# The lower block of a symmetric pair as the transposed image of the upper one, in a graph-convolution kernel

## The chip, the cores and the metric

The kernel runs on one core of one Trainium2 chip. The metric is the device time of one execution in microseconds (us), lower is better. A core has five engines that run side by side, each with its own queue in order: TensorE (PE, with its weight loads as PEld), VectorE (DVE), ScalarE (ACT), GpSimd (POOL) and SyncE (SP, which here only starts DMAs). ACT and POOL start DMAs as well. Matrix products and transposes end in PSUM, and DVE or ACT copies them out to SBUF. The core's DMAs share 16 DMA engines.

## The reference

```python
HW = jnp.einsum('bnf,fo->bno', H, W)            # H = x: (8, 4096, 256), W: (256, 256)
A_norm = jax.nn.relu((A + A.T) * 0.5)           # A = adj: (4096, 4096)
D = jnp.sum(A_norm, axis=1)
d_inv_sqrt = jnp.where(D > 0, D_safe ** (-0.5), 0.0)
DAD = d_inv_sqrt[:, None] * A_norm * d_inv_sqrt[None, :]
L_norm = jnp.eye(N, dtype=H.dtype) - DAD
out = jax.nn.relu(jnp.einsum('nm,bmo->bno', L_norm, HW))
x = layernorm(x + out, axis=-1)
```

All of it is float32. `A_norm` is symmetric: its block (j, i) is the transpose of its block (i, j).

## The kernel before

The work has two stages. The first makes `A_norm`, writes it to DRAM (`a_dram`), makes the rows of HW scaled by their degree (`g`), writes them too (`g_dram`), and forms the first 128 rows of the product on the way (`lead`). The second gathers rows of `g_dram` and pieces of `a_dram` by lists of indices, multiplies them, adds x, normalises and stores the output. The change touches the first stage alone.

**The pair loop (L718 to L768).** A is cut in 8 by 8 blocks of 512x512. A row i of blocks runs j from i to 7; a pair i < j needs two loads of 1 MB on SP, `adj[i,j]` and `adj[j,i]` (L505, four buffers). There are 8 diagonal blocks and 28 pairs: row i has 7 - i pairs. `symmetrise` (L511) makes one block of the sum: for each of its four groups of 128 rows, four 128x128 transposes on PE (L515) fill one PSUM bank (`tr`, of the tag `b0`, four banks), and one addition on DVE (L519) adds the other block out of SBUF and writes 512 columns of `sym`. For a pair it runs twice, once for (i, j) and once for (j, i): 32 transposes and 8 additions. `sym` has three buffers of 1 MB.

**Beside it** run two more things, traced after the two `symmetrise` (L742). `multiply` (L582) is four products of 512 columns for each strip that is ready; they go to four banks of their own. `form` (L595) makes 128 rows of `g`: it loads two pieces of x (L608, or L574 on POOL), transposes them on PE (L615, 16 transposes in four banks of `b0`), copies each bank out on ACT (L616), multiplies by W (L626, 32 products in four banks of `b0`), and copies each bank out on ACT (L636 or L638).

**`keep` (L522)** then runs for each of the two blocks: ACT applies `relu(0.5 * sym)` in place over 2048 columns (L523), DVE sums groups of 32 columns (L526) and those sums again (L531), POOL notes which groups are not empty (L527), ACT starts the store of 1 MB to `a_dram` (L532). `run_due` (L675) after each `keep` does a due piece of work on the index lists, nearly all of it many short DVE instructions with a few products (L241 to L419). It is thickest in rows 2 to 4. During rows 3 and 5 one `sym` buffer is lent to a list (`hot`, L705).

**The order.** A framework puts the traced instructions in each engine's queue ahead of the run, the earlier traced first among those that its own estimate holds ready; the queue itself then runs strictly in order and waits on semaphores. So the queues aren't in the order of the code: additions of the next pair can stand ahead of sums of this one. `tc.issue_after` pins one instruction behind another on its engine (L743, in the last row).

Of the kernel before, what the change touches and what calls it, by code (L numbers as in the profile page):

```python
# [9 lines left out]
F32 = mybir.dt.float32  # L10
AF = mybir.ActivationFunctionType
# [56 lines left out]
def kernel(  # L68
# [25 lines left out]
    nc = tc.nc  # L94
    B, N, F = x.shape
    FO = w.shape[1]
    P = 128
    S = 512
    A = S // P
# [20 lines left out]
    def blocks(u):  # L120

        return min(2, NB - 1 - 2 * u)
# [23 lines left out]
    ident = const.tile([P, P], F32, name="ident")  # L146
# [20 lines left out]
    psum = ctx.enter_context(tc.tile_pool(name="psum", bufs=4, space=bass.MemoryType.PSUM))  # L167
# [322 lines left out]
    with (  # L490
# [12 lines left out]
        def load_adj(i, j):  # L503
            t = blocks_pool.tile([P, A, S], F32, tag="adj", name=f"adj_{i}_{j}")
            nc.sync.dma_start(  # L505
                t,
                adj[i * S : (i + 1) * S, j * S : (j + 1) * S].rearrange("(a p) s -> p a s", p=P),
            )
            return t

        def symmetrise(i, j, tij, tji, sym):  # L511
            for a in range(A):
                pt = psum.tile([P, S], F32, tag="b0", name=f"tr_{i}_{j}_{a}")
                for c in range(A):
                    ins = nc.tensor.transpose(  # L515
                        pt[:, c * P : (c + 1) * P], tji[:, c, a * P : (a + 1) * P], ident
                    )
                done_pe.append(ins.ins)
                nc.vector.tensor_add(sym[:, a, :], pt, tij[:, a, :])  # L519
                yield  # L520

        def keep(i, j, sym, diag):  # L522
            nc.scalar.activation(sym, sym, AF.Relu, scale=0.5)  # L523
            rows = slice(i * A, (i + 1) * A)
            sums = stat1.tile([P, A, S // E], F32, tag="sums", name=f"sums_{i}_{j}", bufs=3)
            nc.vector.tensor_reduce(sums, sym.rearrange("p a (c q) -> p a c q", q=E), AX.X, ALU.add)  # L526
            ins = nc.gpsimd.tensor_scalar(  # L527
                uses[:, rows, j * S // E : (j + 1) * S // E], sums, 0.0, None, ALU.is_gt
            )
            flags.append(ins.ins)  # L530
            nc.vector.tensor_reduce(part[:, rows, j], sums, AX.X, ALU.add)  # L531
            nc.scalar.dma_start(  # L532
                a_dram[i * S : (i + 1) * S, j * S : (j + 1) * S].rearrange("(a p) s -> p a s", p=P), sym
            )
            if i == j:
                for a in range(A):
                    nc.gpsimd.tensor_copy(diag[:, a, :], sym[:, a, a * P : (a + 1) * P])
# [44 lines left out]
        def multiply(m, g, strip):  # L582
            for c in range(G // S):
                nc.tensor.matmul(  # L584
                    lead[c],
                    lhsT=strip,
                    rhs=g[:, c * S : (c + 1) * S],
                    start=not done,
                    stop=len(done) == NB - 1,
                    skip_group_check=True,  # L590
                )
                yield
            done.append(m)
# [63 lines left out]
        def release_all(i):  # L657
            for m in range(i * A, (i + 1) * A):
                if m in held:
                    release(m)  # L660
            lower_diagonal(i, diags.pop(i))
# [5 lines left out]
        def quota(i, j):  # L667

            if i in (2, 3) and j == i:
                return 0  # L670
            return int(j > i or i > 3)
# [3 lines left out]
        def run_due(flush=False):  # L675
            for d in due:
                d[0] -= 1
            while due and (flush or due[0][0] <= 0):
                _, fn, args = due.pop(0)
                fn(*args)  # L680
# [37 lines left out]
        for i in range(NS):  # L718
            diag = stat1.tile([P, A, P], F32, tag="diag", name=f"diag_{i}")
            for j in range(i, NS):  # L720
                tij = load_adj(i, j)
                tji = load_adj(j, i) if j > i else tij
                parts = [(i, j, tij, tji)] + ([(j, i, tji, tij)] if j > i else [])
                parts = [(p, spool.tile([P, A, S], F32, tag="sym", name=f"sym_{p[0]}_{p[1]}")) for p in parts]
                beside = [multiply(*args) for args in waiting]
                waiting.clear()
                products = len(beside)

                for _ in range(quota(i, j)):
                    if known:  # L730
                        beside.append(form(known.pop(0), True, i >= 4))
                    elif early:
                        beside.append(form(early.pop(0), False))
                for p, sym in parts:
                    for _ in symmetrise(*p, sym):
                        pass
                if i == NS - 1:


                    release_all(i - 1)  # L740
                    beside = beside[products:] + beside[:products]
                for n, b in enumerate(beside):  # L742
                    with tc.issue_after(done_pe[-1]) if i == NS - 1 and n < 2 else nullcontext():  # L743
                        for _ in b:
                            pass
                for (rows, cols, _, _), sym in parts:
                    keep(rows, cols, sym, diag)
                    run_due()
            degrees(i)
            diags[i] = diag  # L750
            if i != NS - 2:
                release_all(i)
            known += range(i * A, min((i + 1) * A, NB - HOLD))
            if i in (1, 2, 3, 4):
                u = SEQ[i - 1]
                at = 4 if i == 4 else 1
                gap = 2 if i == 1 else 1
                due += [[at, patterns, (u,)], [at + 1, count_place, (u,)]]
                due += [[at + 1 + (k + 1) * gap, more, (u,)] for k in range(3)]
                if i < 4:  # L760
                    due.append([at + 2 + 3 * gap, count_place_rest, (u,)])
            if i in (2, 4):
                u = SEQ[i // 2 - 1]
                at = 4 if i == 2 else 0
                pieces = spread_early(u)
                due += [[at + k, next, (pieces, None)] for k in (1, 2, 3, 3, 4)]
                due.append([at + 5, collect_index, (u,)])
            due.sort(key=lambda d: d[0])  # L768
# [204 lines left out]
    with (  # L973
# [292 lines left out]
        for q, (u, step) in enumerate(steps):  # L1266
            new = q == 0 or steps[q - 1][0] != u
            if new:
                prepare(u)
                after(4, classify, u)  # L1270
                rows = [2 * u + 1 + b for b in range(2)] if q > 0 and blocks(u) == 2 else []
# [33 lines left out]
            for c in range(NC):  # L1305
                for op in step:
                    rows = slice(0, P) if op[1] is None else slice(op[1] * L, (op[1] + 1) * L)
                    cols = slice(op[3] * E, (op[3] + op[4]) * E)
# [82 lines left out]
```

## Time and profile before

| | us |
|---|---|
| median of 3 runs | 1469.06 (1465.74 to 1475.9) |
| the profiled execution: its own time | 1471.74 |
| its span, first to last instruction | 1470.0 |
| mean granted TensorE clock | 0.978 of full speed |
| PE busy, share of the span | 1382.5, 94% |
| DVE busy | 1025.7, 70% |
| POOL busy | 735.3, 50% |
| ACT busy | 370.8, 25% |

The first stage ends near 586 us: the last instruction of the pair loop runs near 551 us, and then 80 products of `lead` follow. A busy PE is not PE at its peak, since its products are pipelined and their ends are modelled. A wait is put down to the engine or DMA that came last.

### The profile page before, as it was taken

The page shows a single profiled execution, that of the slowest core. Times are in us where ns is not written, and L with a number is a line of the kernel's source. Part 1 is how long each engine was busy: PE and PEld are TensorE (multiplying, and loading weights), DVE is VectorE, ACT ScalarE, POOL GpSimd, SP SyncE. Part 2 cuts the span into 40 slices and gives each one's busy share as a digit, 9 for nine tenths or more (in the row PEclk, how much of TensorE's full clock was granted, in tenths as well). Part 3 has the DMA queues.
Part 4 walks back from the last instruction along what each step waited for, and adds up shares of the span by engine and source line. Part 5 has one row for each costly group of instructions (what it writes and reads, how often), then busy time and mean ns, then how long its engine had stood idle before and what let it go on. Part 6 is the DMA issues. An engine that isn't in the chain of part 4 may idle for free.

```text
span 1470.0 us, 20174 instructions
## 1 busy us (share of the span) xinstructions
PE 1382.5 (94%) x6584; PEld 744.3 (51%) x6584; DVE 1025.7 (70%) x3020; ACT 370.8 (25%) x462; POOL 735.3 (50%) x1521
## 2 busy tenths in 40 slices
PE   7998998979999999999999999998999999999995
PEld 6777877767777774343334333333333333333432
DVE  4667668879787851538659688788879239999544
ACT  4555455544445451010100101100100010101112
POOL 2335001010214244756767777676667647666663
PEclk9999999989999999999999999999999999999998
DMA  9999999999999999979999999999999979999996
GB/s 351 348 369 371 402 389 333 391 379 341 367 362 359 373 375 391 363 300 378 380 412 356 372 402 408 389 353 389 394 386 361 406 276 398 405 391 408 409 384 233
DMA packets 215008, 545.83 MB, mean 371 GB/s; under 512 B 16983, under 2 KB 106647, under 8 KB 179879
## 3 DMA queue, kind: packets, MB, share of 16 engines
q0 software_dynamic: 53552, 287.25, 49.7%
q1 hardware_dynamic: 93200, 126.62, 24.8%
q10 hardware_dynamic: 68144, 130.58, 23.2%
q8 instruction: 55, 0.90, 0.2%
q14 instruction: 57, 0.47, 0.1%
HBM read 426.33 MB, written 136.34 MB: 383 GB/s over the span
## 4 chain that ended last, share of the span: by engine, by line
PE 49%; DMA 26%; DVE 14%; issue 5%; POOL 3%; ACT 2%; POOLq 0%; ACTq 0%; DVEq 0%; SPq 0%
PE py L1254 28%; DMA g<-g_dram,gi 12%; PE pg L626 9%; DMA a_dram<-sym 6%; PE lead L584 5%; DMA ga<-a_dram,ai 4%; DVE sym L519 4%; PE tr L515 3%; DMA xin<-in_x_dram 3%; PE xtr L615 3%; DVE sums L526 2%; POOL ga L1031 1%; ACT sym L523 1%; POOL g L1039 1%; DVE stats L806 1%
## 5 line engine op out<-in xcount | busy, mean ns | idle before, releaser
L1254 PE MATMUL py<-g,ga 128*128 128x512 f32 (+4 forms) x2808 | 659.7, 603 | 16.9 <-DMA g<-g_dram,gi 16.8
L1254 PEld LDWEIGHTS py<-g,ga 128*128 128x128 f32 (+4 forms) x2808 | 233.5, 140 | 408.6 <-issue 379.0
L1039 POOL DMA_INDIRECT g<-g_dram,gi x257 | 289.8, 1128 | 131.6 <-issue 66.1
L1031 POOL DMA_INDIRECT ga<-a_dram,ai x257 | 271.8, 1058 | 146.3 <-issue 50.6
L787 ACT ACTIVATE y<-py,minus_r 128x512 f32<-128x512 f32 x120 | 82.5, 687 | 764.8 <-PE py L1254 725.3
L626 PE MATMUL pg<-w_sb,xt 128*128 128x256 f32 x1024 | 231.8, 385 | 6.0 <-ACT xt L616 6.0
L626 PEld LDWEIGHTS pg<-w_sb,xt 128*128 128x128 f32 x1024 | 196.0, 194 | 33.4 <-ACT xt L616 6.7
L519 DVE TENSOR_TENSOR sym<-tr,adj 128x512 f32<-128x512 f32 x256 | 162.1, 683 | 58.7 <-PE tr L515 50.4
L526 DVE TENSOR_REDUCE sums<-sym 128x64 f32<-128x2048 f32 x64 | 145.6, 2280 | 67.6 <-ACT sym L523 63.5
L1254 PE MATMUL py<-g_hub,gh 128*128 128x512 f32 x384 | 174.4, 601 | 0.0
L527 POOL TENSOR_SCALAR uses<-sums 128x64 uint8<-128x64 f32 x64 | 26.6, 415 | 272.0 <-DVE sums L526 242.0
L515 PE MATMUL tr<-ident,adj 128*128 128x128 f32 x1024 | 137.4, 281 | 20.1 <-DVE sym L519 19.2
L523 ACT ACTIVATE sym<-sym 128x2048 f32<-128x2048 f32 x64 | 122.7, 1918 | 120.5 <-DVE sym L519 108.0
L515 PEld LDWEIGHTS tr<-ident,adj 128*128 128x128 f32 x1024 | 115.7, 143 | 50.8 <-DVE sym L519 36.6
L241 DVE TENSOR_TENSOR_SCAN incl_r<-carry,lists 128x32 f32<-128x32 bf16 x13 | 2.8, 219 | 171.6 <-PE lists L396 171.6
L1254 PEld LDWEIGHTS py<-g_hub,gh 128*128 128x128 f32 x384 | 70.2, 190 | 97.6 <-issue 82.9
L428 DVE TENSOR_TENSOR hot<-iota_q,at 128x1024 bf16<-128x1024 f32 x64 | 74.5, 1218 | 33.8 <-PE lead L584 31.9
L797 DVE TENSOR_TENSOR xr<-xr,y 128x2048 f32<-128x2048 f32 x31 | 70.9, 2287 | 36.9 <-ACT y L787 36.9
L615 PE MATMUL xtr<-ident,xin 128*128 128x128 f32 x512 | 75.2, 301 | 18.3 <-DVE sym L519 11.1
L830 DVE TENSOR_SCALAR xr<-xr,mv,root 128x256 f32<-128x256 f32 x248 | 84.2, 411 | 1.1
L806 DVE BATCH_NORM_STATS2 stats<-xr 128x6 f32<-128x256 f32 x248 | 84.0, 411 | 1.1
L584 PE MATMUL lead<-gt,strip 128*128 128x512 f32 x176 | 82.4, 593 | 0.0
(164 smaller groups left out, 1033.4 us busy)
## 6 DMA issues: line engine op xcount, KB each, us to landing
adj<-in_adj_dram SPq DMA_DIRECT2D x64, 1024.0 KB, 10.7
a_dram<-sym ACTq DMA_DIRECT2D x64, 1024.0 KB, 10.2
out_dram<-xr SPq DMA_DIRECT2D x31, 1024.0 KB, 25.2
xr<-in_x_dram ACTq DMA_DIRECT2D x28, 1024.0 KB, 35.5
xin<-in_x_dram SPq DMA_DIRECT2D x44, 512.0 KB, 10.4
g_dram<-gt ACTq DMA_DIRECT2D x22, 1024.0 KB, 8.1
xin<-in_x_dram POOLq DMA_DIRECT2D x20, 512.0 KB, 6.9
g_dram<-held ACTq DMA_DIRECT2D x10, 1024.0 KB, 11.7
```

The lines of the kernel that those rows point to most:

```text
L515: ins = nc.tensor.transpose(pt[:, c * P : (c + 1) * P], tji[:, c, a * P : (a + 1) * P], ident)
L519: nc.vector.tensor_add(sym[:, a, :], pt, tij[:, a, :])
L523: nc.scalar.activation(sym, sym, AF.Relu, scale=0.5)
L526: nc.vector.tensor_reduce(sums, sym.rearrange("p a (c q) -> p a c q", q=E), AX.X, ALU.add)
L584: nc.tensor.matmul(lead[c], lhsT=strip, rhs=g[:, c * S : (c + 1) * S], start=not done, stop=len(done) == NB - 1, skip_group_check=True,)
L615: nc.tensor.transpose(pt[:, k, c, :], xin[b // H][:, b % H + k, c * P : (c + 1) * P], ident)
L626: ins = nc.tensor.matmul(pg[:, k * FO : (k + 1) * FO], lhsT=xt[:, b + k, c, :], rhs=w_sb[:, c, :], start=(c == 0), stop=(c == FC - 1),)
L806: nc.vector.bn_stats(stats[:, b, :], z[:, b, :])
L830: nc.vector.tensor_scalar(z[:, b, :], z[:, b, :], mv[:, b, 0:1], rstd[:, b : b + 1], ALU.subtract, ALU.mult,)
L1031: nc.gpsimd.indirect_dma_start(out=at if both else at[:, : E if one else P], out_offset=None, in_=a_pairs if both else a_groups if one els ...
L1039: nc.gpsimd.indirect_dma_start(out=gt, out_offset=None, in_=g_dram, in_offset=bass.IndirectOffsetOnAxis(ap=gi[:, t : t + 1], axis=0), boun ...
L1254: return nc.tensor.matmul(py[2 * u + 1 + b][c][cols, :], lhsT=at[ps, off + cols.start : off + cols.stop], rhs=gt[ps, c * S : (c + 1) * S], ...
```

## The change

`symmetrise` runs once for a pair. The relu moves from `keep` to its end. `keep` and `run_due` for (i, j) move ahead of the work beside. After that work the new function `mirror` transposes the finished block (i, j) into `b0` banks on PE, and ACT copies each bank into a `sym` buffer, `low`, that is taken only then; `keep` for (j, i) follows without a relu. The diagonal blocks have no mirror.

```diff
                     )
                 done_pe.append(ins.ins)
                 nc.vector.tensor_add(sym[:, a, :], pt, tij[:, a, :])
-                yield
+            nc.scalar.activation(sym, sym, AF.Relu, scale=0.5)
+
+        def mirror(i, j, upper, sym):
+            for a in range(A):
+                pt = psum.tile([P, S], F32, tag="b0", name=f"mirror_{i}_{j}_{a}")
+                for c in range(A):
+                    nc.tensor.transpose(
+                        pt[:, c * P : (c + 1) * P], upper[:, c, a * P : (a + 1) * P], ident
+                    )
+                nc.scalar.copy(sym[:, a, :], pt)
 
         def keep(i, j, sym, diag):
-            nc.scalar.activation(sym, sym, AF.Relu, scale=0.5)
...
-                parts = [(i, j, tij, tji)] + ([(j, i, tji, tij)] if j > i else [])
-                parts = [(p, spool.tile([P, A, S], F32, tag="sym", name=f"sym_{p[0]}_{p[1]}")) for p in parts]
+                sym = spool.tile([P, A, S], F32, tag="sym", name=f"sym_{i}_{j}")
                 beside = [multiply(*args) for args in waiting]
...
-                for p, sym in parts:
-                    for _ in symmetrise(*p, sym):
-                        pass
+                symmetrise(i, j, tij, tji, sym)
+                keep(i, j, sym, diag)
+                run_due()
                 if i == NS - 1:
...
-                for (rows, cols, _, _), sym in parts:
-                    keep(rows, cols, sym, diag)
+                if j > i:
+                    low = spool.tile([P, A, S], F32, tag="sym", name=f"sym_{j}_{i}")
+                    mirror(j, i, sym, low)
+                    keep(j, i, low, diag)
                     run_due()
```

## Rows read from the trace of the kernel before

**Rows 1.** The page: busy time of each engine over the whole span.
```profile
PE 1382.5 (94%) x6584; PEld 744.3 (51%) x6584; DVE 1025.7 (70%) x3020; ACT 370.8 (25%) x462; POOL 735.3 (50%) x1521
```
**Rows 2.** Windows: the pair loop by rows of blocks (0, 1, 2, 3, 4, 5 to 7).
```profile
core 0: us, PE busy (x) PEld busy (x) DVE busy (x) ACT busy (x) POOL busy (x), PEclk, DMA share, GB/s
0.00:121.00 121.00, 107.21 (x619) 90.10 (x620) 74.17 (x113) 62.84 (x78) 44.41 (x701) 0.99 1.00 353
121.00:222.00 101.00, 93.90 (x526) 76.55 (x525) 65.94 (x92) 50.99 (x62) 21.93 (x119) 0.97 1.04 392
222.00:304.00 82.00, 76.34 (x427) 61.01 (x426) 68.24 (x150) 41.86 (x46) 5.38 (x15) 0.96 1.01 369
304.00:379.00 75.00, 64.70 (x332) 51.25 (x331) 65.85 (x142) 32.71 (x38) 11.68 (x23) 0.89 0.93 339
379.00:444.00 65.00, 63.44 (x372) 50.09 (x371) 48.54 (x112) 32.06 (x40) 15.34 (x29) 1.00 1.01 380
444.00:551.00 107.00, 101.00 (x547) 78.52 (x546) 76.24 (x158) 54.03 (x65) 37.13 (x63) 0.98 0.99 371
```
**Rows 3.** Waits in 222 to 379 us: us in total, times, longest us.
```profile
ACT sym L523 <- DVE sym L519: 42.3, 12, 6.5
PEld tr L515 <- DVE sym L519: 21.7, 23, 5.0
PE tr L515 <- DVE sym L519: 14.8, 10, 4.8
```
**Rows 4.** Timeline, 303 to 310 us: start us, us, engine and line.
```profile
303.34 0.69 DVE L519 TENSOR_TENSOR sym<-tr,adj 128x512 f32<-128x512 f32 x1 [0.98 <-PE tr L515]
303.95 4.47 DVE L526 TENSOR_REDUCE sums<-sym 128x64 f32<-128x2048 f32 x2
...
308.68 0.68 DVE L519 TENSOR_TENSOR sym<-tr,adj 128x512 f32<-128x512 f32 x1
...
309.40 4.67 PE L515 MATMUL tr<-ident,adj 128*128 128x128 f32 x20 [4.79 <-DVE sym L519]
```
**Rows 5.** Groups by line: count, busy us, mean ns, idle before.
```profile
L519 DVE TENSOR_TENSOR sym<-tr,adj 128x512 f32<-128x512 f32 x256 | 162.1, 683 | 58.7 <-PE tr L515 50.4 <-DMA a_dram<-sym 3.5 <-DMA adj<-in_adj_dram 2.2
L526 DVE TENSOR_REDUCE sums<-sym 128x64 f32<-128x2048 f32 x64 | 145.6, 2280 | 67.6 <-ACT sym L523 63.5 <-POOL group_of L224 4.2
L523 ACT ACTIVATE sym<-sym 128x2048 f32<-128x2048 f32 x64 | 122.7, 1918 | 120.5 <-DVE sym L519 108.0 <-DMA g_dram<-gt 12.5
L616 ACT COPY xt<-xtr 128x512 f32<-128x512 f32 x128 | 67.9, 594 | 55.7 <-PE xtr L615 54.8 <-ACT held L651 0.4
L636 ACT ACTIVATE gt<-pg,r 128x512 f32<-128x512 f32 x88 | 60.6, 689 | 65.1 <-PE pg L626 61.3 <-PE pr L396 3.1 <-issue 0.7
```
**Rows 6.** Chain of waits, 465 to 481 us: an unbroken stretch of PE.
```profile
465.34 3.67 PE tr L515 x32
469.01 3.44 PE lead L584 x8
472.45 1.75 PE xtr L615 x16
474.19 6.91 PE pg L626 x32
```
**Rows 7.** Chain of waits: its start, and one turn of row 0.
```profile
0.81 4.70 DMA xin<-in_x_dram
...
72.26 8.96 DMA a_dram<-sym
81.21 1.80 DVE sym L519 x3
83.04 1.91 ACT sym L523
84.95 1.23 ACT xt L616 x3
```
**Rows 8.** Windows: an unbroken stretch of row 1, columns as in rows 2.
```profile
150.00:210.00 60.00, 58.69 (x339) 48.53 (x338) 33.94 (x43) 31.12 (x39) 3.77 (x9) 1.00 1.05 403
```

## The prediction

> **What bounds the kernel now.** I read the busy times first, then the first stage cut by rows of blocks, then the waits and the timeline of the worst rows, then the chain of waits. Over the whole span PE is busy 94% and DVE 70% [rows 1], which says little, since the change touches only the pair loop, 0 to 551 us of 1470. In the cut by rows of blocks [rows 2] the reader should look at three columns. PE is nearly full in rows 4 to 7 (63.44 of 65 us, 101.00 of 107) and has its gaps in row 0 (13.8 us idle, 5.6 of them the first load of x, which nothing precedes [rows 7]), row 1 (7.1) and rows 2 and 3 (5.7 and 10.3). DVE is at 61%, 65%, 83%, 88%, 75% and 71%: it peaks just where PE has the most gaps, and there the granted clock is lowest too, 0.96 and 0.89 of full speed: part of the time PE ran at 1.2 GHz in place of 2.4. The DMA column stands near 1.00 everywhere.
>
> The waits of rows 2 and 3 name the link: PE stood 14.8 us before transposes for an addition of `symmetrise` to free a bank, and its weight loads 21.7 us [rows 3]; most of the second lies inside the first or under running products, so I don't add them. The timeline shows how one looks. At 303.34 an addition runs; then two sums of 2.28 us each stand ahead of the next addition, which comes at 308.68; PE's transposes had waited 4.79 us for it [rows 4]. Where DVE is not ahead of PE's need, nothing of this happens: from 465 us PE runs 15.8 us of transposes, `lead`, x transposes and products without a gap [rows 6].
>
> **Part by part.**
>
> *DVE.* Removed are 28 x 4 = 112 additions of 0.683 us [rows 5]: 76.5 us of its 399 in the pair loop [rows 2]. Nothing is added: sums and list work stay. Rows 2 and 3 hold 9 pairs, so 36 additions, 24.6 us of 68.24 + 65.85 = 134.1 [rows 2]; DVE there goes from 85% to 70% of today's 157 us.
>
> *PE.* The mirror has 16 transposes for the 16 that go, 448 in all, no change in work. Its operand is `sym` instead of `adj`, both float32 in SBUF.
>
> *ACT.* Removed are 28 relus of 1.918 us, 53.7 us; added are 112 copies out of PSUM. The nearest rows are the x copies, same shape, at 0.594 us, and the scaled copies at 0.689 [rows 5]: 66.5 to 77.2 us. I take 0.594, since it is a plain copy as well. ACT gets 13 us more (13 to 24), on 275 us busy in 551 us [rows 2]. That is no bound as a sum. Its order is what may matter, below.
>
> *The added wait.* The mirror's transposes wait on PE for the relu; behind them stand the next pair's transposes. The relu is traced ahead of the work beside, which is 1.75 + 6.91 us of `form` and 1.72 us a strip of `lead` [rows 6]; addition and relu after the last transposes need 0.68 + 1.92 = 2.6 us, so I cost this wait at nothing. Without that cover (a pair with no `form`) it costs up to 2.6 us; by the code the rows that `form` may take run short in at most three or four pairs. The mirror's banks are freed at 0.594 us apiece where PE fills one in 3.67 / 8 = 0.46 us, and the last product bank still has its 0.69 us copy ahead: PE falls behind by 4 x 0.135 + 0.69 = 1.2 us a pair. Under `lead`, which needs no bank of `b0`, that is hidden; row 0 has no `lead`, and pays it.
>
> *Moved.* The relu, sums and store of block (i, j) go ahead of the work beside; the store of (j, i) comes after it. On ACT's queue the store of (i, j) is issued in front of the evictions of `form` and not behind them, a place or two of 0.37 us each, which is no term. The two `adj` buffers of a pair come free after one `symmetrise`, so SP's loads, and the x loads that queue behind them, can start some microseconds sooner. I put no number on it: no row of PE's waits above is for `adj`. POOL's notes follow the sums as before.
>
> *The `sym` buffers.* In row 0 one turn is a store of 8.96 us, three additions 1.80, the relu 1.91 and three copies of x that stand before the next store, 1.23: 13.9 us [rows 7], against 1.75 + 6.91 + 3.67 = 12.3 us of PE work [rows 6]. With three buffers a pair's second block waits for the store of the first block of the pair before. Today that first block is stored late, behind the work beside, and the second block is needed early. After the change the first is stored early and the second needed late: the gate opens most of a turn sooner. What is late next is PE with the 1.2 us of bank turnover: 12.3 + 1.2 = 13.5, a gain of 0.4 us a pair, 1.6 if the turnover hides. Over six pairs that is 2 to 10 us; I take 2.
>
> *Rows 2 and 3.* What PE can win at most is its idle time and its missing clock [rows 2]: 5.7 + 10.3 idle and 0.04 x 82 + 0.11 x 75 = 11.5 us of clock, 27.5 in all. The granted clock fell in stretches that follow PE's gaps, so it should come back with them. At least it wins nothing. With half of the bank evictions that DVE served now on ACT, and DVE at 70%, most of the waits like that of rows 4 should go; sums of 2.28 us ahead of an addition remain. I take 16 of 27.5, which sets 157 us to 141.
>
> *Row 1 and rows 4 to 7.* Idle there is 7.1 and 7.6 us [rows 2], in many small pieces, while DVE is at 65% to 75%. I take 2 and 1, between 0 and 14.7.
>
> *Sum.* 16 + 2 + 2 + 1 = 21 us off the profiled execution's 1471.74 (span 1470.0 and 1.7 around it): 1450.7. The shown median is 2.7 us below that execution, so 1448 against 1469.06. The 919 us after 551 move up and are otherwise not touched.
>
> *Is there room in the DMAs?* The pair loop moves the same bytes. Summing rate by time [rows 2] gives 202.4 MB at 367 GB/s; in 530 us it would be 382, and in rows 2 and 3, 355 (the mean of the two) x 157 / 141 = 395 GB/s. Row 1 held 403 GB/s for 60 us with PE 58.69 of 60 busy [rows 8]. So the trace shows a higher rate than I need, if narrowly. The Trainium skill, "DMA: Bandwidth & Descriptors", section "Where 436 GB/s comes from", says that between HBM and SBUF a core's share of HBM, about 358 GB/s, binds, against 435 for the fabric. By that rule the pair loop could not get below 202.4 / 0.358 = 565 us (an estimate from that page), no gain at all. The 403 GB/s above speaks against it here; "Perfetto Trace Analysis", section "Roofline", says a core running alone can pass that share, up to about 120% of it, which fits.
>
> **The rivals.**
>
> *The DMAs are the floor.* For it: their share is 0.99 or more in every row of blocks but row 3 [rows 2], and every store that PE waits out through `sym` takes 9 us. Then only the slack of row 3 can be won, 0.07 x 75 = 5 us: 1464. Against it: the same share of 1.00 went with 353 GB/s in row 0 and 1.05 with 403 in row 1, so a share of one isn't a fixed rate. This is the case in which the rule of the DMA page above would hold, and also what comes out if the DVE waits merely change their name.
>
> *ACT becomes the gate, and it gets slower.* The place is ACT's queue after the first half of a pair. The relu waits there for the last addition, and the x copies that PE's products need stand behind it. From the last transposes: addition 0.68, relu 1.92, copy 0.59 is 3.2 us, against 1.75 us of x transposes: PE stands 1.4 us, and with the 1.2 us of turnover 2.7 us a pair (the parts unrounded). If half of the 28 pairs pay it, that is 38 us less the 21 won, 17 us slower: 1486. It decides from 21 / 2.7 = 8 pairs on. For it: ACT already waits 42.3 us in two rows with a relu at its head [rows 3], and its queue is in order. Against it: `lead` lasts 1.72 us a strip and covers from row 1 on, and the order lets x copies that are ready go ahead of the relu.
>
> *More than I take.* If DVE's waits vanish as a class, rows 0 to 3 give their whole idle time and clock: 27.5 + 8.2 + 7.1 = 43 us, so 1426. For it: the unbroken stretch of rows 6 exists already where DVE was less busy. Against it: x loads and row starts account for some of the idle time and remain, and 367 x 551 / 508 = 398 GB/s would have to hold throughout.
>
> **How the numbers follow.** Forecast 0.50, with its own range of 1437 to 1459 (10 us of gain to 32). DMA floor 0.22, ACT gate 0.14, more 0.14. The range takes half of the last case and goes past the floor, 1427 to 1475, and leaves the ACT case out. About 1% is what a measurement of this kernel can tell from no change, 14.7 us, bounds 1454.4 and 1483.8. Faster: 0.14 and 0.42 of the forecast's 0.50, 0.56. Slower: 0.13 of the ACT case. Same: the rest, 0.31.
>
> **What would show it.** Right: DVE's additions 256 to 144, its busy time down by 76 us; rows 2 and 3 shorter by some 16 us with a granted clock near 1; waits of transposes for additions below a third of today's; no chain through a store of `sym` in row 0; mirror copies near 0.6 us. Wrong: PE waiting for x copies or for the mirror's copies by more than 1 us in most pairs (ACT gate); PE's waits now for loads or stores with the stage at 365 to 370 GB/s (DMA floor); or a gain in the pair loop that doesn't reach the end.

## The result and the profile after

The kernel after takes 1481.76 us (median of 8 runs, 1477.43 to 1486.64), the kernel before, beside it on the same chip, 1472.72 us (8 runs, 1465.74 to 1475.9). The ratio is 1.0071, 95% interval 1.0045 to 1.0098: slower by 0.7%, where 1.5% faster was forecast. The profiled execution took 1480.02 us, its span is 1478.2, its mean granted clock 0.980. The second stage is untouched: from its first product to the end it takes 884.3 us before and 884.0 after. The last product of `form`, which ends the pair loop, starts at 551.2 us before and at 559.6 after. So the whole loss of the profiled execution, 8.2 us of span, is in the loop.

New lines after the change: `tr` transposes L515, addition L519, relu L520, mirror transposes L526, mirror copy L529, sums L534, store L540, x transposes L623, x copy L624, products of `form` L634.

The page's busy line of the kernel after answers to [rows 1]:

```profile
PE 1372.4 (93%) x6584; PEld 739.7 (50%) x6584; DVE 965.4 (65%) x2908; ACT 377.1 (26%) x546; POOL 738.9 (50%) x1521
```

DVE gave up 60.3 us and ACT took on 6.3. The groups by line of the kernel after answer to [rows 5] (count, then busy us, mean ns of one, and the idle time before them with what ended it):

```profile
L534 DVE TENSOR_REDUCE sums<-sym 128x64 f32<-128x2048 f32 x64 | 145.9, 2279 | 23.8 <-ACT sym L520 23.7
L519 DVE TENSOR_TENSOR sym<-tr,adj 128x512 f32<-128x512 f32 x144 | 94.5, 686 | 157.2 <-PE tr L515 148.0 <-DMA a_dram<-sym 9.2
...
L520 ACT ACTIVATE sym<-sym 128x2048 f32<-128x2048 f32 x36 | 69.0, 1918 | 103.4 <-DVE sym L519 103.4
...
L529 ACT COPY sym<-mirror 128x512 f32<-128x512 f32 x112 | 58.5, 598 | 3.7 <-PE mirror L526 3.7
L526 PE MATMUL mirror<-ident,sym 128*128 128x128 f32 x448 | 55.4, 278 | 4.5 <-ACT sym L520 4.5
```

The work moved as written: 112 additions fewer, 28 relus fewer, 112 copies of 598 ns. The idle time in front of the additions is new: 58.7 us in [rows 5], 157.2 now, nearly all of it for transposes. DVE now waits for PE more than it did, and still PE's idle time in the loop grew: from 44.4 us (the windows of [rows 2] added up) to 61.3 (those below).

The windows of the kernel after by rows of blocks, cut where each row's last store is issued, answer to [rows 2]:

```profile
core 0: us, PE busy (x) PEld busy (x) DVE busy (x) ACT busy (x) POOL busy (x), PEclk, DMA share, GB/s
0.00:119.50 119.50, 102.51 (x634) 92.27 (x635) 57.58 (x89) 65.49 (x101) 44.88 (x701) 0.99 1.02 371
119.50:222.00 102.50, 94.52 (x528) 76.65 (x527) 51.88 (x67) 52.83 (x79) 21.84 (x118) 0.97 1.02 379
222.00:312.00 90.00, 73.85 (x401) 58.09 (x400) 60.04 (x134) 41.08 (x59) 5.95 (x17) 0.93 0.97 355
312.00:390.00 78.00, 68.31 (x396) 54.49 (x394) 58.35 (x127) 36.81 (x54) 13.12 (x27) 0.93 0.92 335
390.00:456.00 66.00, 63.40 (x350) 49.65 (x346) 45.50 (x116) 32.88 (x49) 15.32 (x28) 1.00 1.00 376
456.00:560.00 104.00, 96.08 (x519) 73.90 (x518) 68.34 (x127) 52.93 (x70) 34.02 (x61) 0.98 0.98 367
```

Row 2 is the place: 90 us where it was about 80, with 16 us of PE idle and a clock of 0.93 for 0.96. DVE's share there fell to 67%, so the queue that I had called too full is less full, and PE waits more. The waits of rows 2 and 3 after (us in total, times, longest) answer to [rows 3]:

```profile
ACT sym L520 <- DVE sym L519: 46.1, 10, 6.9
...
PE tr L515 <- DVE sym L519: 8.5, 6, 1.9
...
PE tot L299 <- DVE kind L289: 6.7, 1, 6.7
...
PE mirror L526 <- ACT sym L520: 4.5, 1, 4.5
```

The old wait, transposes for additions, fell from 14.8 to 8.5 us. Two single waits took its place: 6.7 us of a list's product (`tot`) for a table that DVE makes, and 4.5 us of the mirror for the relu.

To see where the loop's length comes from, one table for all kernels: the length in us of rows 0 to 3 of blocks (each to the issue of its last store), of rows 4 to 7 together (from there to the end of the loop), and the end of the loop, all in one profiled execution of each, and the ratio of the times. In the kernels measured later the second stage took 905 to 924 us in place of 884, so the loop is compared by its own end, and the whole time only by the ratio to the kernel before that was measured beside it. The same code twice ("after" and "after again") differs by 3 us at the loop's end and up to 2.5 us in a row; less than that I don't read.

| kernel | row 0 | row 1 | row 2 | row 3 | rows 4-7 | loop ends | ratio |
|---|---|---|---|---|---|---|---|
| before | 122.4 | 101.9 | 79.9 | 76.4 | 170.5 | 551.2 | 1 |
| after | 119.5 | 102.7 | 90.1 | 78.0 | 169.4 | 559.6 | 1.0071 |
| after_again | 117.9 | 100.2 | 90.3 | 78.1 | 170.1 | 556.6 | 1.0067 |
| due_back | 119.7 | 102.8 | 86.6 | 75.0 | 171.8 | 555.9 | 1.0026 |
| mirror_alone | 119.5 | 99.6 | 86.6 | 75.4 | 170.9 | 552.1 | 1.0010 |
| moves_alone | 111.3 | 100.8 | 83.9 | 75.8 | 169.1 | 540.9 | 0.9940 |
| moves_due_back | 111.1 | 101.4 | 82.4 | 79.5 | 176.7 | 551.1 | 0.9987 |
| dve_copies | 130.7 | 107.3 | 88.9 | 75.1 | 173.1 | 575.2 | 1.0161 |
| sums_later | 123.9 | 102.2 | 86.7 | 82.7 | 171.5 | 567.1 | 1.0107 |
| relu_late | 117.6 | 98.2 | 86.5 | 77.1 | 174.0 | 553.4 | 1.0047 |
| both_late | 113.1 | 101.8 | 81.2 | 75.5 | 170.2 | 541.7 | 0.9966 |
| all_three | 112.2 | 101.4 | 83.8 | 75.5 | 171.1 | 544.0 | 0.9960 |
| mirror_early | 111.4 | 102.6 | 88.0 | 70.8 | 177.2 | 550.1 | 1.0004 |
| mirror_rows23 | 110.4 | 100.2 | 83.5 | 70.9 | 173.9 | 538.9 | 0.9914 |

### The profile page after: what moved, and what is told of

It reads as the page before. It is cut to its first block, busy times and chain, and to the rows that moved or that the text cites. A ratio compares the mean times of both kernels' runs of the same rounds, so it can differ in the third digit from the quotient of the medians.

```text
span 1478.2 us, 20093 instructions
## 1 busy us (share of the span) xinstructions
PE 1372.4 (93%) x6584; PEld 739.7 (50%) x6584; DVE 965.4 (65%) x2908; ACT 377.1 (26%) x546; POOL 738.9 (50%) x1521
## 4 chain that ended last, share of the span: by engine, by line
PE 53%; DMA 18%; DVE 18%; issue 6%; POOL 3%; ACT 1%; POOLq 0%; ACTq 0%; DVEq 0%
PE py L1263 28%; PE pg L634 12%; DMA g<-g_dram,gi 10%; PE lead L592 6%; DVE sums L534 3%; DMA ga<-a_dram,ai 3%; PE xtr L623 3%; PE tr L515 2%; PE mirror L526 2%; DVE sym L519 2%; DMA a_dram<-sym 2%; POOL g L1048 1%; POOL ga L1040 1%; DMA adj<-in_adj_dram 1%; DVE hot L428 1%
## 5 line engine op out<-in xcount | busy, mean ns | idle before, releaser
L1048 POOL DMA_INDIRECT g<-g_dram,gi x257 | 293.2, 1141 | 125.3 <-issue 63.7
L1040 POOL DMA_INDIRECT ga<-a_dram,ai x257 | 275.0, 1070 | 145.1 <-issue 51.0
L796 ACT ACTIVATE y<-py,minus_r 128x512 f32<-128x512 f32 x120 | 82.7, 689 | 764.3 <-PE py L1263 683.3
L634 PE MATMUL pg<-w_sb,xt 128*128 128x256 f32 x1024 | 234.3, 388 | 7.7 <-ACT xt L624 7.7
L634 PEld LDWEIGHTS pg<-w_sb,xt 128*128 128x128 f32 x1024 | 196.1, 194 | 37.2 <-ACT xt L624 9.5
L519 DVE TENSOR_TENSOR sym<-tr,adj 128x512 f32<-128x512 f32 x144 | 94.5, 686 | 157.2 <-PE tr L515 148.0
L534 DVE TENSOR_REDUCE sums<-sym 128x64 f32<-128x2048 f32 x64 | 145.9, 2279 | 23.8 <-ACT sym L520 23.7
L623 PE MATMUL xtr<-ident,xin 128*128 128x128 f32 x512 | 71.2, 292 | 26.9 <-DVE sym L519 16.4
L520 ACT ACTIVATE sym<-sym 128x2048 f32<-128x2048 f32 x36 | 69.0, 1918 | 103.4 <-DVE sym L519 103.4
L806 DVE TENSOR_TENSOR xr<-xr,y 128x2048 f32<-128x2048 f32 x31 | 70.8, 2285 | 35.6 <-ACT y L796 30.5
L515 PE MATMUL tr<-ident,adj 128*128 128x128 f32 x576 | 78.3, 279 | 15.0 <-DVE sym L519 14.5
L515 PEld LDWEIGHTS tr<-ident,adj 128*128 128x128 f32 x576 | 64.6, 142 | 42.0 <-DVE sym L519 36.8
## 6 DMA issues: line engine op xcount, KB each, us to landing
out_dram<-xr SPq DMA_DIRECT2D x31, 1024.0 KB, 24.6
```

The lines of the kernel that those rows point to most:

```text
L515: ins = nc.tensor.transpose(pt[:, c * P : (c + 1) * P], tji[:, c, a * P : (a + 1) * P], ident)
L623: nc.tensor.transpose(pt[:, k, c, :], xin[b // H][:, b % H + k, c * P : (c + 1) * P], ident)
L634: ins = nc.tensor.matmul(pg[:, k * FO : (k + 1) * FO], lhsT=xt[:, b + k, c, :], rhs=w_sb[:, c, :], start=(c == 0), stop=(c == FC - 1),)
L1040: nc.gpsimd.indirect_dma_start(out=at if both else at[:, : E if one else P], out_offset=None, in_=a_pairs if both else a_groups if one els ...
L1048: nc.gpsimd.indirect_dma_start(out=gt, out_offset=None, in_=g_dram, in_offset=bass.IndirectOffsetOnAxis(ap=gi[:, t : t + 1], axis=0), boun ...
```

## The experiments

The first two theories came from the waits above. **A**: the list work, started earlier, puts itself and its products in front of the pairs. **B**: ACT's queue is the gate, since relu, mirror copies and x copies stand in one line.

**The list work back behind the work beside.** `keep` of the first block stays early.

```diff
                 keep(i, j, sym, diag)
-                run_due()
...
                         for _ in b:
                             pass
+                run_due()
                 if j > i:
```

> The changed kernel with the first call of the list work (run_due) put back behind the work beside, ahead of the mirror; all else as changed. Theory A, the early list work stands in PE's and DVE's queues ahead of the pair's own work (the 6.7 us wait of a list product in row 2): the 7 to 10 us come back, about 1473, level with the kernel before, and row 2 loses its 6.7 us wait. Theory B, ACT's queue is the gate, with relu and mirror copies: no change, about 1481. Theory C, the sums of the mirrored block standing between the next pair's additions: no change, about 1481.

Measured: ratio 1.0026 (1.0011 to 1.0041), loop to 555.9. The 6.7 us wait for `kind` is gone from the trace of rows 2 and 3, which are 3.5 and 3.0 us shorter; row 0 is as it was. So A holds for these two rows and for 0.4% of the time (1.0067 or 1.0071 less 1.0026), and not for the rest.

**The mirror without the moves.** `keep` and `run_due` of the first block both go behind the work beside, as before the change.

```diff
                 symmetrise(i, j, tij, tji, sym)
-                keep(i, j, sym, diag)
-                run_due()
...
+                keep(i, j, sym, diag)
+                run_due()
                 if j > i:
```

> The changed kernel with keep and run_due of the upper block both behind the work beside, so that the mirror and the early relu alone are left of the change. Theory A: at or below the kernel before, 1465 to 1473. Theory B: as slow as the changed kernel, 1478 to 1484. Theory C: 1478 to 1484 as well, since both sums now come at the turn of the pair.

Measured: ratio 1.0010 (0.9995 to 1.0025), loop to 552.1. With 112 additions fewer the kernel is no faster than with them, and nearest to what theory A had; B and C, which had it as slow as the changed kernel, miss. Row 0 is 2.9 us shorter than in the kernel before, but rows 2 and 3, where most of the gain was forecast, are 5.7 us longer (162.0 for 156.3).

**The moves without the mirror.** The kernel before, with `keep` and `run_due` of the first block ahead of the work beside; all additions stay.

```diff
+                keep(i, j, parts[0][1], diag)
+                run_due()
                 if i == NS - 1:
...
-                for (rows, cols, _, _), sym in parts:
+                for (rows, cols, _, _), sym in parts[1:]:
```

> The kernel before with its two symmetrise and all its additions, but with relu, keep and run_due of the first block put ahead of the work beside; no mirror. Theory A: slower than before by most of what the change lost, 1479 to 1484. Theories B and C, which blame the mirror: no slower than before, 1465 to 1473.

Measured: ratio 0.994 (0.9921 to 0.9959), loop to 540.9: the side effect of the change is the gain, and the mirror, on top of it, costs 16 to 19 us of loop. Theory A, which had this kernel slower than before, misses here. Neither part loses time alone (loops of 540.9 and 552.1 against 551.2); the loss comes when both are there. 11 us of the gain stand in row 0, where the stores through `sym` no longer set the turn. The loop moved its bytes faster, too; the window of its first 541 us in this kernel, columns as above:

```profile
0.00:541.00 541.00, 496.60 (x2814) 403.33 (x2815) 405.85 (x768) 276.31 (x324) 140.18 (x950) 0.97 1.02 376
```

So the DMAs were no floor at 367 GB/s.

**The mirror's copies on DVE.**

```diff
-                nc.scalar.copy(sym[:, a, :], pt)
+                nc.vector.tensor_copy(sym[:, a, :], pt)
```

> The changed kernel with the mirror's banks copied by VectorE in place of ScalarE, 112 copies of some 0.6 us. Theory B: faster than the changed kernel, 1470 to 1477, the turn in rows with lead back from 16.0 to 15.8 us. Theories A and C: slower than the changed kernel, 1483 to 1492, since DVE gets its 70 us back in the rows where list work is thick.

Measured: ratio 1.0161 (1.0138 to 1.0185), loop to 575.2, and a turn of row 0 of 14.9 to 16.5 us where the kernel after has 14.3. It is slower than any of the theories had it. B in its plain form falls: with 58.5 us of copies taken off ACT the loop is longer. The copies are better where the change put them.

What then holds PE in row 0? The timeline of one turn of the kernel after, first PE, then DVE, then ACT (start us, us):

```profile
73.89 1.91 PE L526 MATMUL mirror<-ident,sym 128*128 128x128 f32 x16
75.64 1.91 PE L515 MATMUL tr<-ident,adj 128*128 128x128 f32 x16
77.39 0.60 PE L623 MATMUL xtr<-ident,xin 128*128 128x128 f32 x4
79.81 1.53 PE L623 MATMUL xtr<-ident,xin 128*128 128x128 f32 x12 [1.83 <-DVE sym L519]
...
76.28 0.69 DVE L519 TENSOR_TENSOR sym<-tr,adj 128x512 f32<-128x512 f32 x1 [4.51 <-PE tr L515]
76.88 2.28 DVE L534 TENSOR_REDUCE sums<-sym 128x64 f32<-128x2048 f32 x1
79.08 0.68 DVE L519 TENSOR_TENSOR sym<-tr,adj 128x512 f32<-128x512 f32 x1
...
80.50 1.08 ACT L624 COPY xt<-xtr 128x512 f32<-128x512 f32 x2 [1.90 <-PE xtr L623]
81.47 1.92 ACT L520 ACTIVATE sym<-sym 128x2048 f32<-128x2048 f32 x1
```

DVE idles 4.51 us, makes one addition, and then the sums of the mirrored block, finished a moment ago, stand ahead of the second. The x transposes need the bank which that addition frees, and wait 1.83 us. The chain of waits of the kernel after shows that this is the turn, again and again (start us, us, what):

```profile
59.79 1.75 PE mirror L526 x16
61.54 0.45 PE tr L515 x4
61.99 0.02 issue
62.01 0.42 DVE sym L519
62.43 0.19 issue
62.62 2.28 DVE sums L534
64.89 0.61 DVE sym L519
65.50 0.04 issue
65.55 1.53 PE xtr L623 x12
67.08 6.98 PE pg L634 x32
74.05 1.75 PE mirror L526 x16
```

From 59.79 to 74.05 it is 14.26 us. PE's own work in it is 3 x 1.75 + 6.91 = 12.2. So **theory C**: sums of the mirrored block stand between the next pair's additions. I ran the kernel after again beside two tests.

**The kernel after, once more.** No edit.

> The changed kernel as it is, beside the next two on one chip, so that they are compared with it under the same conditions. Every theory: 0.4% to 1.0% slower than the kernel before, pair loop ending near 560 us, row 0 with a turn of 14.3 us.

Measured: ratio 1.0067 (1.0043 to 1.0092), loop to 556.6. The slowdown is there again, beside another measurement of the kernel before.

**The mirrored block's sums behind the next pair's additions.** Its sums, its notes on POOL and its part of the degrees (as `note`) are traced after the next `symmetrise` and pinned behind its last addition.

```diff
...
                 symmetrise(i, j, tij, tji, sym)
+                while behind:
+                    with tc.issue_after(added[-1]):
+                        note(*behind.pop())
...
```

> The changed kernel with one thing moved: the sums and the POOL note of the mirrored block are traced behind the next pair's four additions and pinned behind the last of them on DVE. Theory C, the mirrored block's sums of 2.28 us stand between the next pair's additions because the mirror comes last in the turn: the turn of row 0 falls from 14.3 to 13.2 to 13.6 us, the pair loop ends 8 to 15 us sooner, the whole 0.5% to 1% below the changed kernel. Theory B, ACT's queue with relu and copies is the gate: turn and total as the changed kernel, within 3 us. Theory A, only the early list work costs: as the changed kernel, within 3 us, with the 6.7 us wait of row 2 still there.

Measured: ratio 1.0107 (1.0081 to 1.0132), loop to 567.1: worse. The timeline of this kernel, ACT and then PE, shows why:

```profile
65.29 1.91 ACT L520 ACTIVATE sym<-sym 128x2048 f32<-128x2048 f32 x1 [2.16 <-DVE sym L519]
67.11 0.57 ACT L632 COPY xt<-xtr 128x512 f32<-128x512 f32 x1
...
63.89 2.09 PE L631 MATMUL xtr<-ident,xin 128*128 128x128 f32 x16
67.73 4.54 PE L642 MATMUL pg<-w_sb,xt 128*128 128x256 f32 x12 [1.76 <-ACT xt L632]
```

The additions now run together (2.48 us from 62.78), the x transposes go through without a wait, and the relu, ready at once, gets in front of the x copies. PE waits 1.76 us there, and 18.3 us in ten such waits over the loop, where the kernel after has 7.7 in two. The 12 products behind the wait took 4.54 us; the granted clock was 0.62 from 67.7 to 70.7 us, after PE had stood, and 1.00 ahead of it. C's forecast of a shorter turn fails, and so does B's of an unchanged total.

The windows of the whole loop, of the kernel after and then of this one (columns as above), show where the 7 us that it is longer lie:

```profile
0.00:560.00 560.00, 498.68 (x2815) 405.05 (x2816) 341.69 (x656) 282.02 (x408) 135.14 (x950) 0.97 0.99 365
0.00:567.00 567.00, 507.69 (x2813) 411.09 (x2814) 341.82 (x656) 281.29 (x408) 135.16 (x950) 0.95 0.98 361
```

PE's idle time is the same or less, 59.3 us for 61.3: one wait took the place of the other. What grew is its busy time, 507.7 for 498.7 us on the same work, at a granted clock of 0.95 for 0.97. So what makes this kernel the slower of the two is PE's clock, and not more waiting.

**The mirror between the x transposes and the products of `form`**, so that products follow it in place of the next pair's transposes.

```diff
...
+                if j > i:
+                    for n, b in enumerate(beside):
+                        for _ in b if n < products else range(4):
+                            if n >= products:
+                                next(b)
+                    low = spool.tile([P, A, S], F32, tag="sym", name=f"sym_{j}_{i}")
+                    mirror(j, i, sym, low)
...
```

> The changed kernel with the mirror, its keep and run_due traced between the x transposes and the products of form, not behind them, so that its sums run beside the products. Theory C: 8 to 18 us below the changed kernel, turn of row 0 near 13.2 us. Theory B: slower than the changed kernel by 10 us and more, since PE now waits for the relu before the mirror in every pair without lead, some 1 to 1.5 us each. Theory A: within 3 us of the changed kernel.

Measured: ratio 1.0004 (0.9991 to 1.0018), loop to 550.1, 6 to 10 us better than after, as theory C had it; B, which had it slower, misses. Row 0 is 111.4 us and row 3 is 70.8, both far shorter than before; rows 4 to 7 take 177.2 and give 7 us of it back. The mirror now waits for the relu in earnest: 11.1 us in eight waits.

From these **theory D**: after the change the head of a turn has 16 transposes in place of 32 (the mirror's 16 stand at the end of the turn). What is left covers too little: the additions, the relu and the x copies now run in series, so one of them is always late. Lifting the sums alone shows the relu, as above; lifting the relu alone should show the sums; only both at once should help.

**The relu behind the x copies.** The relu of the upper block, with its `keep`, is traced after the x transposes and pinned behind the last x copy on ACT.

```diff
...
+        def half(sym):
             nc.scalar.activation(sym, sym, AF.Relu, scale=0.5)
...
+                with tc.issue_after(copied[-1]) if after else nullcontext():
+                    half(sym)
                 keep(i, j, sym, diag)
```

> The changed kernel with the relu of the upper block pinned on ACT behind the x copies of the pair's form, the mirrored block's sums where the change has them. Theory D: the sums still stand between the additions, turn of row 0 14.3 us as before, total as the changed kernel, 1.004 to 1.009. Theory B, the relu in front of the x copies is the whole cost: turn 13.2 us, 0.995 to 1.001.

Measured: ratio 1.0047 (1.002 to 1.0073), loop to 553.4. Row 0 (117.6) stays where it was, and so does its turn: 14.26 us in the chain, with the sums between the additions, as D had it. The loop's end alone would have promised a better ratio, but this profiled execution has a second stage of 923.6 us against 908 to 915 in the kernels measured beside it, for which I have no cause.

**Both.** The two edits above together.

```diff
...
+                while behind:
+                    with tc.issue_after(added[-1]):
+                        note(*behind.pop())
...
+                with tc.issue_after(copied[-1]) if after else nullcontext():
+                    half(sym)
```

> The changed kernel with two things moved: the mirrored block's sums behind the next pair's additions, as in sums_later, and the relu of the upper block pinned on ACT behind the four x copies of the pair's form. Theory D, the mirror leaves PE only the 16 transposes and the x transposes to run while additions, relu and x copies follow each other, so that either the sums or the relu is in the way and lifting one alone shows the other: the turn of row 0 falls to 13.2 to 13.6 us, loop 5 to 15 us shorter than the changed kernel's, total level with the kernel before, 0.995 to 1.001. Theory B with ACT too busy as such: turn stays at 14.3 us or more, 1.005 to 1.012.

Measured: ratio 0.9966 (0.9948 to 0.9984), loop to 541.7. Alone the edits gave 1.0107 and 1.0047, together 0.9966, 15 to 18 us off the loop of the kernel after, more than the 5 to 15 that D had. The chain of waits in this kernel:

```profile
49.98 1.06 PE xtr L635 x8
51.04 6.91 PE pg L646 x32
57.95 1.75 PE mirror L530 x16
59.70 1.75 PE tr L515 x16
61.44 0.89 PE xtr L635 x8
62.33 0.02 issue
62.35 13.41 DMA xin<-in_x_dram
...
75.89 1.07 PE xtr L635 x8
```

PE runs its 12.3 us without a gap, and the next thing late is a load of x. From 49.98 to 75.89 are two turns, so a turn is 13.0 us, where each edit alone left it above 14. In row 0 that is D. In rows 2 and 3, 11 to 12 us shorter than in the kernel after, a second thing is mixed in: with the relu the first list work, too, is traced behind the x transposes, and the wait for `kind` is down from 6.7 us to 0.8. Over the first 541 us PE is busy 495.0 us here, so 46.0 idle, near the 44.4 of the moves alone in the window above.

**The mirror in rows 2 and 3 alone**, placed early as above, on top of the moves; rows 0, 1 and 4 to 7 keep their additions. It asks what the 36 additions that I priced at 16 us are worth.

```diff
...
+                if j > i and i not in (2, 3):
+                    low = spool.tile([P, A, S], F32, tag="sym", name=f"sym_{j}_{i}")
+                    symmetrise(j, i, tji, tij, low, False)
...
+                if j > i and i in (2, 3):
...
+                    mirror(j, i, sym, low)
...
```

> The kernel of moves_alone (additions for both blocks, first block kept early), with the mirror in rows 2 and 3 alone, traced early as in mirror_early: there DVE is busiest. If 36 additions fewer on DVE are worth what was forecast for those rows: rows 2 and 3 10 to 16 us shorter than in moves_alone (159.6 us there), total 0.983 to 0.988. If PE's gaps in those rows have another cause, such as diagonal blocks that have no form to run beside them: within 5 us of moves_alone, 0.991 to 0.998.

Measured: ratio 0.9914 (0.9894 to 0.9935), loop to 538.9. Rows 2 and 3 take 154.4 us against 159.7 with the moves alone, the whole difference in row 3; rows 4 to 7, the same code, take 4.8 more. So they are 5.3 us shorter and not 10 to 16. This is the fastest kernel of the study, faster than the one with both edits (0.9966, measured beside it). That it is faster than the moves alone isn't shown: the intervals around 0.9914 and 0.994 overlap, and the two weren't measured side by side.

**The moves alone, with the list work back.**

```diff
                 keep(i, j, parts[0][1], diag)
-                run_due()
...
+                run_due()
                 for (rows, cols, _, _), sym in parts[1:]:
```

> The kernel of moves_alone with the first list work put back behind the work beside. Theory A as it is left, early list work costs by itself: 2 to 6 us faster than moves_alone, 0.990 to 0.992. If it costs only where PE has nothing else ready at the head of the turn, as after the mirror: as moves_alone, 0.992 to 0.996, with the turn of row 0 at 13.2 us in both.

Measured: ratio 0.9987 (0.9969 to 1.0004), loop to 551.1. Row 0 keeps its gain (111.1), so that comes from `keep`, as forecast from [rows 7]; rows 3 to 7 lose 11 us. Neither expectation had that. Early list work helps where the additions stay (0.994 against 0.9987) and hurts in the kernel after (1.0071 against 1.0026).

**All three edits of the order**: both late, and the list work back.

```diff
                 keep(i, j, sym, diag)
-                run_due()
...
+                run_due()
                 if j > i:
```

> The changed kernel with all three of the order's edits: the relu behind the x copies, the mirrored block's sums behind the next pair's additions (these two together gave a loop of 541.7 us and 0.9966), and the first of the two calls for list work traced behind the work beside (alone 555.9 against 559.6 us, and 1.0026 against 1.007). Theory A and D together (what the early list work costs in rows 2 and 3 is a separate wait, for the kind and position tables, not covered by either of the other two edits): another 3 to 6 us off, the loop at 536 to 539 us and a ratio of 0.992 to 0.995. Rival, D alone (with the series of addition, relu and x copy lifted, the early list work does no harm, as it did none with additions, where it helped by 10 us): the loop at 541 to 550 us and a ratio of 0.996 to 1.0.

Measured: ratio 0.996 (0.9941 to 0.998), loop to 544.0; rows 2 and 3 are no shorter than with both late. That is the rival's result, D alone: moving the list work further back gains nothing more. It doesn't show that list work ahead of the x transposes would be harmless in this order, since both late had already moved it behind them. Whether it hurt in the kernel after only because of the series stays open.

## Why the prediction was wrong

**The step that failed is the one in "Rows 2 and 3": "I take 16 of 27.5, which sets 157 us to 141".** They took 168.1. I had seen DVE's share peak where PE had its gaps [rows 2] and read the one as the cause of the other. The trace of after takes that apart: DVE's share there fell from 85% to 70%, and PE's idle time in the two rows rose from 16.0 us to 25.8. That 70% is the figure I had written is luck: DVE's busy time fell by 15.7 us where I had 24.6, and the rows grew. The clock didn't come back either: 0.93 in both rows is 11.8 us of missing clock for today's 11.5. PE's new waits here come from the order of work in in-order queues, not from more of it. One is in pair (2,7), which has no `form` beside it; the timeline of the kernel after, ACT and PE:

```profile
306.00 1.91 ACT L520 ACTIVATE sym<-sym 128x2048 f32<-128x2048 f32 x1 [6.91 <-DVE sym L519]
...
307.96 3.67 PE L526 MATMUL mirror<-ident,sym 128*128 128x128 f32 x16 [4.51 <-ACT sym L520]
```

I had priced this at up to 2.6 us in three or four pairs; it took 4.51, because the sums of the mirrored block stood between the additions here too, as in [rows 4], and the mirror then ran at half clock (3.67 us for 1.91; granted clock 0.50, its level of 1.2 GHz, from 308 to 312). The other is the 6.7 us for `kind`: DVE was busy through all 8 us from 226 to 234 with additions, sums and the tables of the list work that the change had moved forward. I had listed `run_due` nowhere among the moved steps and so gave it no price. Where the mirror stands earlier, it is worth about 5 us in these rows, its own waits included (moves alone against the mirror in rows 2 and 3), a third of my figure and not far above the noise of a row.

**"I cost this wait at nothing"** was the second fault. I checked the cover of the mirror's own wait and found it under `form`. But the 16 transposes that became the mirror had themselves been a cover: at the head of a turn PE had run them while the additions and the relu went on. Moved to the end of the turn they cover nothing there, and additions, sums, relu and x copies come out in series. I wrote that "sums of 2.28 us ahead of an addition remain", and gave them no price: they are 2.28 of the 14.26 us of every turn of row 0 above. In all, the loop of the kernel after is 16 to 19 us longer than with the moves alone; moving the sums and the relu out of the way gives 15 to 18 back, with the list work's wait among them. The 1.2 us a pair of bank turnover that I had row 0 pay showed nowhere: in the loop of the kernel after PE has no wait for a mirror copy.

**The `sym` buffers.** The mechanism was right and the size was off. Today's gate of 8.96 us of store [rows 7] stands four times in the chain of waits between 10 and 110 us of the kernel before, once in that of the kernel after (10.74 us from 21.01), and not at all with the moves alone. I took 2 us, from a range to 10: with additions it is worth 11 us (122.4 to 111.3 and 111.1). In the kernel after the series took most of it back: row 0 is 119.5, and its turn of 14.26 us is no shorter than the 13.9 of before.

**DVE and ACT.** Both terms were too large, since I multiplied by the mean duration of one. Consecutive additions overlap, so 112 fewer are 162.1 - 94.5 = 67.6 us of busy time and not 76.5; the copies cost 58.5 us and not 66.5. The mean of a copy, 598 ns, is the 594 that I took. Neither term stands in the sum, so neither error moved the forecast.

**The rivals.** "ACT becomes the gate" had the right direction, and half of the reason. Its pair of relu and x copies costs what it said (1.4 us worked out, 1.76 measured), but only once the sums are out of the way; in the kernel after DVE's queue is late first, and this rival's time of 1486 was nearer than mine. That its copies are dear fell with dve_copies. "The DMAs are the floor" fell: 376 GB/s held over the shorter loop. The Trainium skill, "DMA: Bandwidth & Descriptors", section "Where 436 GB/s comes from", has about 358 GB/s bind; the loops here ran past it, so the measurement decides. "More than I take" fell with the forecast: DVE's share went down and PE's waits did not.

The bound of my range, 1475 us, left out the ACT case; a case with a mechanism and a price of 2.7 us a pair over 28 pairs should have been inside it.

The Trainium skill, "Perfetto Trace Analysis", section "Optimizing Scalar/DVE Operations", says that moving some work off DVE may make sense if DVE is saturated, and that breaking instructions up may help where an engine isn't saturated but causes gaps on others. Row 0 of the kernel after is the second case: DVE is busy 57.58 of 119.5 us, 48%, and it is the length and place of one sum that PE waits for. No run here breaks the sums up.

**What stays open.** The lengths of rows 4 to 7 differ by 8 us among the kernels (169.1 to 177.2) without an edit there in some of them; I read it as due list work that lands elsewhere, but no run tells that apart.

## What to carry to other kernels

Before you move work off an engine, ask what PE's wait is for: a full engine, or an instruction in the wrong place of an in-order queue. A busy share can't tell them apart; the timeline of two turns can. When work moves from the head of a turn to its end, list what it had been covering, and add up in series what now runs bare. When a change bundles moves with a replacement, run each alone and both: here the moves alone gained 0.6%, the replacement alone cost nothing that shows, and together they lost 0.7%.

## What the runs showed of the hardware

A store that is held on ACT's queue holds the copies behind it, which have nothing to do with it. In pair (1,4) of the kernel after, timeline of ACT and then PE:

```profile
160.19 0.57 ACT L624 COPY xt<-xtr 128x512 f32<-128x512 f32 x1
165.34 0.37 ACTq L540 DMA_DIRECT2D a_dram<-sym  x1
165.74 1.57 ACT L624 COPY xt<-xtr 128x512 f32<-128x512 f32 x3 [4.99 <-DMA adj<-in_adj_dram]
...
166.38 4.91 PE L634 MATMUL pg<-w_sb,xt 128*128 128x256 f32 x15 [3.58 <-ACT xt L624]
```

The relu that makes that store's data was over at 160.3, and yet the store went out 5 us later, when a load of `adj`, under way for 19.4 us, landed; three copies of x stood behind it on ACT, and PE stood 3.58 us. From its first transpose to the next pair's, this pair takes 21.3 us here, 15.7 before and 16.0 with the mirror alone, so the wait isn't there in every order. With the moves alone it takes 20.4, but there PE waits 2.8 us for a load of x. Why the store waited for a load on another queue isn't settled by these runs.

The second stage, the same instructions in every kernel, took 884 us in the first two profiles and 905 to 924 in the later ones, which were taken on three chips. Which chip the first two were taken on isn't on record, so no run shows whether the chip is the cause.
